# Four graph layers on one core: the y tiles of layer 0 in three long runs between inner products

## The chip, the cores and the metric

The kernel runs on one core of a Trainium2 chip, in one launch. The metric is the device time of that launch in microseconds (us). TensorE (PE) multiplies matrices; PEld is its loading of weights, which goes on beside the multiplications. VectorE (DVE), ScalarE (ACT) and GpSimd (POOL) work on elements. SyncE (SP) issues most of the DMAs. Each engine works through its own queue in order and waits on semaphores.

## The reference

x has 8 batches of 2048 nodes with 64 features; adj is a dense 2048 x 2048 matrix. Everything is float32. Four layers follow each other, each as `x = layernorm(x + layer(x, adj))`:

```python
# layer 0: for each node n its own weights, mixed from 16 sets by the node's embedding
w = einsum('nd,dkio->nkio', embedding, weight);  b = einsum('nd,do->no', embedding, bias)
As = [I, A, 2 * A @ A - I]
out = einsum('bnki,nkio->bno', einsum('knm,bmc->bnkc', stack(As), x), w) + b
# layer 1: twice  z = relu((A z) W_i)
# layer 2: x W_self + (A x) W_neighbor + bias
# layer 3: [x, A x, 2 A A x - x, A x, 2 A A x - x] W + bias
```

Every layer needs products with A, and layer 0 in addition needs for every node and batch a product with the 16 weight sets (`y` in the kernel), summed with the 16 numbers of the node's embedding.

## The kernel before

**Layout.** The tile `xy` in SBUF holds two slots of the node features: 128 partitions by 16 node tiles by 2 slots by 512 columns (8 batches of 64 features, in 4 pairs `p`). A first part (lines 500 to 715) computes A x for layer 0, puts it in slot 1, keeps its transpose in DRAM (`t1T`), and prepares sums of blocks of A for what follows (`comb`, in DRAM).

**A product with A.** From then on `product` does every product, six in all: layer 0's T2 = A (A x), then A z twice in layer 1, once in layer 2 and twice in layer 3. It is a Strassen-like scheme on two levels. The outer level has seven products of halves, named A11, S1, A12, S2, S4, S3, A22 in the order in which they run, on quarters of the features or on sums of them (`T`, made by `t1` to `t4`). Each of the seven is a call of `inner`, which has again seven block products (`mul`). A block product loads one 1 MB block of A or of its sums (`load`, tile `a`, a ring of four buffers; from layer 1's A12 on, three more in `ring2`, which lies in the memory that layer 0's tiles leave), and multiplies it in four matmuls of 128 x 128 by 128 x 512 into one PSUM bank: `mma`, `mmb` or `mmc`. There are two banks in layer 0, used in turn, so the third accumulation of an inner product takes the bank that the first has just left. VectorE adds the partial results: `u2`, `u3`, then the results (`C`), and before each inner product the four sums of its features (`t`).

**The y tiles.** T2's results come out in quarters: (0,0) after A12, (0,1) after S4, (1,1) after S3, (1,0) after A22, four tiles of 512 nodes by one pair of batches in each. As soon as a tile is there, `hand_over` gives a generator `feature0` (line 770) to the pump. For each of its four node tiles it runs two halves: 12 matmuls with 64 rows (the two batches of a pair side by side in the array) put 2 x 512 numbers into a PSUM tile `y` (three buffers). VectorE adds the first half's eight parts into `xy`, each scaled by the embedding (line 800); ScalarE scales the second half's eight parts into `s` (line 804); GpSimd sums them and adds the sum into `xy` (lines 809 and 811). `fetch` loads xT and tT of the tile ahead through SyncE's queue.

**Layer norm.** When two neighbouring pairs of a group of nodes are done, `then` puts the layer norm of these columns on a list of deferred work (`defer`, with a gap of 4 steps). It squares on GpSimd (`sq`, line 365), reduces on VectorE (`ss`, line 371), takes a square root on ScalarE (line 376) and scales `xy` (line 381).

**The pump.** `pump.step` is called after every block product and lets pending generators go on. For layer 0 the rate is 4 and the batch 16: after every four block products, 16 steps are done, which is two y tiles. `mark` notes the last tile of quarter (0,1); `pass_mark`, at the start of the next product, runs the pump to there. The tiles that are left run within layer 1's A11 and S1, after which `drain` empties the pump and `between` (`to_late`) frees layer 0's memory, PSUM included.

**What sets the order.** The program is written in one stream. A scheduler then gives each engine its order: by the place in the stream, but an instruction that is ready may go ahead of others that wait. `tc.keep_in_program_order` pins an instruction. Waits are put in after that.

Of the kernel before, what the change touches and what calls it, by code (L numbers as in the profile page):

```python
# [22 lines left out]
A11, A12, A22, S1, S2, S3, S4 = range(7)  # L23
# [6 lines left out]
class Pump:  # L30


    def __init__(self):
        self.jobs = []
        self.later = []
        self.rate = 1
        self.gate = None
        self.owed = 0
        self.batch = 1

    def add(self, gen):
        self.jobs.append(gen)
# [22 lines left out]
    def tick(self, idle=False):  # L65
        for job in list(self.later):

            job[0] -= 0.5 if idle and job[4] else 1
            if job[0] <= 0:
                job[0], job[4] = job[1], False  # L70
                if next(job[2], "done") == "done":
                    self.later.remove(job)

    def step(self, n=1, now=False):
        self.owed += n
        if self.jobs and self.owed < self.batch and not now:
            return
        n, self.owed = int(self.owed), self.owed - int(self.owed)
        while n > 0 and (self.jobs or self.later):
            try:  # L80
                idle = not self.jobs
                if not idle:
                    next(self.jobs[0])
                n -= 1
                self.tick(idle)
            except StopIteration:
                self.jobs.pop(0)
# [8 lines left out]
def kernel(  # L96
# [18 lines left out]
    nc = tc.nc  # L115
# [73 lines left out]
            nc.sync.dma_start(a, comb[q][s].rearrange("p (n m c) -> p n m c", n=TG, m=TG))  # L189
        return a  # L190

    def product(src, feature, between=None, rate=1, own=None, pin=False, batch=1):

# [8 lines left out]
        def new_t():  # L204
            return sums.tile([P, NT // 2, 4 * F], F32, tag="T", name="T", bufs=3)
# [4 lines left out]
        def inner(q, b, finish, early=None):  # L210


            b11, b12, b21, b22 = (
                b[:, hm * TG : (hm + 1) * TG, ts(hc, 2 * F)] for hm in range(2) for hc in range(2)
            )

            def new():
                return sums.tile([P, TG, 2 * F], F32, tag="t", name="t", bufs=5)

            t1 = add(new(), b12, b11, ALU.subtract)  # L220
            t2 = add(new(), b22, t1, ALU.subtract)
            t3 = add(new(), b22, b12, ALU.subtract)
            t4 = add(new(), b21, t2, ALU.subtract)

            def mul(ps, s, xb, start, stop=True):
                a = load(q, s)
                for m in range(TG):
                    nc.tensor.matmul(  # L228
                        ps, xb[:, m, :], a[:, :, m, :], start=(start and m == 0),
                        stop=(m == TG - 1), skip_group_check=True,  # L230
                    )
                pump.step(pump.rate)

            def bank(n):
                nonlocal banks
                banks += 1
                pool = p_mm if p_mm2 is None or banks % 3 else p_mm2
                return pool.tile([P, GW], F32, tag="mm", name=f"mm{n}")

            pa, pb = bank("a"), bank("b")  # L240
            mul(pa, 0, b11, True)
            p1 = sums.tile([P, GW], F32, tag="p1", name="p1")
            nc.scalar.copy(p1, pa)  # L243
            if early is not None:
                early(2, p1)
            mul(pb, 5, t2, True)
            u2 = add(sums.tile([P, GW], F32, tag="u2", name="u2"), pb, p1)
            if early is not None:
                early(1, u2)
            mul(pa, 1, b21, False)  # L250
            finish(0, pa, None)
            mul(pb, 6, t3, False)
            u3 = add(sums.tile([P, GW], F32, tag="u3", name="u3"), pb, p1)
            if early is not None:
                early(3, u3)
            pc = bank("c")
            mul(pc, 4, t1, True)
            finish(3, pc, u3)
            mul(pb, 3, t4, False)
            finish(2, pb, p1)  # L260
            mul(pc, 7, b22, False)
            finish(1, pc, u2)

        def fresh(c):
            def finish(blk, ps, plus):
                if plus is None:
                    nc.scalar.copy(c[:, blk, :], ps)
                else:
                    add(c[:, blk, :], ps, plus)
            return finish,  # L270

        def onto(c, base, give=None, then=None):

            def early(blk, plus):
                add(c[:, blk, :], base[:, blk, :], plus)

            def finish(blk, ps, plus):
                add(c[:, blk, :], ps, (base if plus is None else c)[:, blk, :])
                if give is not None:
                    hand_over(c, *give, blk)  # L280
                if then is not None:
                    then(blk)
            return finish, early
# [16 lines left out]
        if pin:  # L300
            tc.keep_in_program_order(sub)
        inner(A11, b11, *fresh(u))
        inner(S1, t1, *fresh(v))
        pump.drain()
        pump.rate, pump.batch = rate, batch
        if between is not None:
            between()
        t2 = new_t()
# [3 lines left out]
        prior(0, 0)  # L312
        c = new_c()
        inner(A12, b21, *onto(c, u, (0, 0)))
        t3 = new_t()
        sub = nc.vector.tensor_tensor(t3, b22, b12, ALU.subtract)
        if pin:
# [3 lines left out]
        prior(1, 0)  # L321
        c = new_c()
        inner(S2, t2, *onto(u, u, then=lambda blk: add(c[:, blk], u[:, blk], v[:, blk])))
        inner(S4, b22, *onto(c, c, (0, 1)))
        pump.mark()
        prior(1, 1)

# [2 lines left out]
            hand_over(v, 1, 1, blk)  # L330

        inner(S3, t3, *onto(u, u, then=last))
        inner(A22, t4, *onto(u, u, (1, 0)))

    def to_nodes(dst, pool, tiles, p, hT):
# [72 lines left out]
    if True:  # L408
# [347 lines left out]
        if True:  # L756
            p_y = first.enter_context(tc.tile_pool(name="p_y", bufs=3, space=PSUM))
            l0y = first.enter_context(tc.tile_pool(name="l0y", bufs=1))
            e_sb = l0y.tile([P, NT, D], F32, tag="e_sb", name="e_sb")
            nc.gpsimd.dma_start(e_sb, emb)  # L760


            order = [
                (2 * ih + k // 2, 2 * ch + k % 2)
                for ih, ch in ((0, 0), (0, 1), (1, 1), (1, 0)) for k in DONE
            ]
            fetched = {}

            def fetch(k):
                if k < len(order):  # L770
                    i, p = order[k]
                    fetched[i, p] = [l0y.tile([P, GW], F32, tag=n, name=n, bufs=2) for n in ("xT", "tT")]
                    for tile_, src in zip(fetched[i, p], (xT, t1T)):
                        nc.sync.dma_start(tile_, src[p][:, ts(i, GW)])

            def feature0(g, p, hT):
                if (g, p) == order[0]:
                    fetch(0)
                fetch(order.index((g, p)) + 1)
                terms = fetched.pop((g, p)) + [hT]  # L780
                for k in range(TG):
                    t = g * TG + k
                    acc = xy[:, t, 0, ts(p, 2 * F)].rearrange("p (b f) -> p b f", f=F)


                    s = l0y.tile([P, DH, 2, F], F32, tag="s", name="s", bufs=2)
                    for h in range(2):
                        y = p_y.tile([P, 2, DH * F], F32, tag="y", name="y")
                        for n in range(3):
                            for b in range(2):  # L790
                                half = slice(b * F, (b + 1) * F)
                                nc.tensor.matmul(  # L792
                                    y[:, b, :], terms[n][half, ts(k, P)],
                                    wn[half, n, h * DH : (h + 1) * DH, :],
                                    start=(n == 0), stop=(n == 2),
                                )
                        for d in range(DH):
                            e = e_sb[:, t, h * DH + d : h * DH + d + 1]
                            if h == 0:
                                nc.vector.scalar_tensor_tensor(  # L800
                                    acc, y[:, :, ts(d, F)], e, acc, ALU.mult, ALU.add
                                )
                            else:
                                nc.scalar.activation(s[:, d], y[:, :, ts(d, F)], AF.Copy, scale=e)  # L804
                        if h == 0:
                            yield
                    n = DH // 2
                    while n:
                        nc.gpsimd.tensor_tensor(s[:, :n], s[:, :n], s[:, n : 2 * n], ALU.add)  # L809
                        n //= 2  # L810
                    nc.gpsimd.tensor_tensor(acc, acc, s[:, 0], ALU.add)
                    yield

            product(1, then(feature0, 0, gap=4, pool_sq=True), rate=4, batch=16)


    late = p_z = None
# [134 lines left out]
```

## Time and profile before

Three runs took 1692.46, 1690.90 and 1686.34 us, median 1690.9. The profiled execution took 1690.62 us, its span from the first to the last instruction is 1688.8.

| | us | share of the span |
|---|---|---|
| time of the profiled execution | 1690.62 | |
| its span | 1688.8 | |
| TensorE busy | 1666.1 | 99% |
| weight loads | 856.5 | 51% |
| VectorE busy | 942.0 | 56% |
| ScalarE busy | 265.3 | 16% |
| GpSimd busy | 249.6 | 15% |
| y matmuls in the chain of waits | | 19.5% |
| matmuls of products (`mma`, `mmb`, `mmc`) in the chain | | 57.7% |

The granted clock of TensorE was 0.996 of full speed. The y tiles run between 225 and 752 us: the first part ends at about 220 us, layer 1's S1 begins at 752.

In the profile a line of the chain of waits has start, length, engine, tile and line of the kernel, and the number of records. One float32 matmul shows as two records, so a block product is x8, one y tile x96. A line of the timeline has start, length, engine, line, operation and shapes, and in brackets how long the engine had been idle and what ended it.

### The profile page before, as it was taken

The page shows a single profiled execution, that of the slowest core. Times are in us where ns is not written, and L with a number is a line of the kernel's source. Part 1 is how long each engine was busy: PE and PEld are TensorE (multiplying, and loading weights), DVE is VectorE, ACT ScalarE, POOL GpSimd, SP SyncE. Part 2 cuts the span into 40 slices and gives each one's busy share as a digit, 9 for nine tenths or more (in the row PEclk, how much of TensorE's full clock was granted, in tenths as well). Part 3 has the DMA queues.
Part 4 walks back from the last instruction along what each step waited for, and adds up shares of the span by engine and source line. Part 5 has one row for each costly group of instructions (what it writes and reads, how often), then busy time and mean ns, then how long its engine had stood idle before and what let it go on. Part 6 is the DMA issues. An engine that isn't in the chain of part 4 may idle for free.

```text
span 1688.8 us, 16180 instructions
## 1 busy us (share of the span) xinstructions
PE 1666.1 (99%) x5952; PEld 856.5 (51%) x5952; DVE 942.0 (56%) x1687; ACT 265.3 (16%) x763; POOL 249.6 (15%) x332
## 2 busy tenths in 40 slices
PE   9899999999999999999999999999999999999997
PEld 4588854444444444444455455554444455554443
DVE  5477884546456656454443365863557444543556
ACT  0000000332323332330011010220001011100001
POOL 1122200443344544450000000000000000000000
PEclk9999999999999999999999999999999999999999
DMA  9898978134333123309877877667888866678883
GB/s 326 328 353 329 331 275 303 62 123 166 109 114 123 52 86 125 112 19 376 303 268 264 310 253 257 226 216 283 291 296 282 306 210 237 231 265 309 316 310 121
DMA packets 82271, 391.25 MB, mean 232 GB/s; under 512 B 8880, under 2 KB 25264, under 8 KB 42640
## 3 DMA queue, kind: packets, MB, share of 16 engines
q1 hardware_dynamic: 69504, 346.78, 58.4%
q0 software_dynamic: 11248, 42.08, 6.5%
q10 hardware_dynamic: 1440, 1.35, 0.2%
q8 instruction: 48, 0.79, 0.2%
q14 instruction: 31, 0.25, 0.0%
HBM read 339.85 MB, written 50.33 MB: 231 GB/s over the span
## 4 chain that ended last, share of the span: by engine, by line
PE 95%; DVE 3%; DMA 1%; POOL 0%; ACT 0%; issue 0%; POOLq 0%; DVEq 0%
PE mmb L228 25%; PE y L792 20%; PE mmc L228 17%; PE mma L228 16%; PE ps_n L655 8%; PE ps_n L618 3%; PE z L840 2%; PE z L872 2%; DMA a<-in_slices 1%; PE pt L831 1%; PE pt L889 1%; DVE ss L371 0%; PE pt_n L339 0%; DVE xy L381 0%; DVE sm L355 0%; DVE xy L356 0%
## 5 line engine op out<-in xcount | busy, mean ns | idle before, releaser
L228 PE MATMUL mmb<-a,t 128*128 128x512 f32 x1008 | 454.9, 593 | 1.1 <-DVE xy L381 1.1
L228 PEld LDWEIGHTS mmb<-a,t 128*128 128x128 f32 x1008 | 188.7, 190 | 229.0 <-issue 224.7
L800 DVE SCALAR_TENSOR_TENSOR xy<-y,e_sb,xy 128x128 f32<-128x128 f32 x512 | 179.7, 351 | 137.5 <-PE y L792 121.6
L809 POOL TENSOR_TENSOR s<-s 128x512 f32<-128x512 f32 (+2 forms) x192 | 159.0, 828 | 339.5 <-ACT s L804 329.3
L804 ACT ACTIVATE s<-y,e_sb 128x128 f32<-128x128 f32 x512 | 138.9, 382 | 270.5 <-PE y L792 270.4
L228 PE MATMUL mma<-a,T 128*128 128x512 f32 x384 | 173.3, 594 | 0.0
L201 DVE TENSOR_TENSOR u<-mmb,p 128x512 f32<-128x512 f32 x84 | 58.0, 690 | 193.8 <-PE mmb L228 188.4
L228 PE MATMUL mmc<-a,t 128*128 128x512 f32 x336 | 151.7, 594 | 0.0
L792 PE MATMUL y<-wn,xT 64*128 64x512 f32 x512 | 133.1, 592 | 0.0
L228 PE MATMUL mma<-a,xy 128*128 128x512 f32 x288 | 130.4, 594 | 2.7 <-DVE C L201 2.6
L792 PE MATMUL y<-wn,tT 64*128 64x512 f32 x512 | 131.3, 589 | 0.0
L792 PE MATMUL y<-wn,C 64*128 64x512 f32 x512 | 131.2, 589 | 0.0
L228 PEld LDWEIGHTS mma<-a,T 128*128 128x128 f32 x384 | 71.4, 190 | 84.3 <-issue 83.5
L201 DVE TENSOR_TENSOR C<-mmc,C 128x512 f32<-128x512 f32 x60 | 41.4, 690 | 101.7 <-PE mmc L228 101.7
L228 PEld LDWEIGHTS mmc<-a,t 128*128 128x128 f32 x336 | 61.9, 190 | 70.9 <-issue 70.4
L228 PEld LDWEIGHTS mma<-a,xy 128*128 128x128 f32 x288 | 53.8, 190 | 68.6 <-issue 62.9
L228 PE MATMUL mmc<-a,T 128*128 128x512 f32 x192 | 86.4, 593 | 0.0
L243 ACT COPY p<-mma 128x512 f32<-128x512 f32 x42 | 24.5, 584 | 377.8 <-PE mma L228 375.8
L792 PEld LDWEIGHTS y<-wn,xT 64*128 64x128 f32 x512 | 49.2, 187 | 63.3 <-issue 62.9
L792 PEld LDWEIGHTS y<-wn,tT 64*128 64x128 f32 x512 | 49.5, 187 | 60.6 <-issue 60.6
L792 PEld LDWEIGHTS y<-wn,C 64*128 64x128 f32 x512 | 49.6, 187 | 60.3 <-issue 60.3
L228 PE MATMUL mmc<-a,xy 128*128 128x512 f32 x144 | 64.9, 593 | 0.0
(114 smaller groups left out, 1587.9 us busy)
## 6 DMA issues: line engine op xcount, KB each, us to landing
a<-comb SPq DMA_DIRECT2D x240, 1024.0 KB, 4.8
a<-in_blocks SPq DMA_DIRECT2D x54, 1024.0 KB, 4.9
comb<-si POOLq DMA_DIRECT2D x28, 1024.0 KB, 10.9
a<-in_slices SPq DMA_DIRECT2D x15, 1024.0 KB, 8.2
comb<-so POOLq DMA_DIRECT2D x16, 512.0 KB, 5.7
comb<-so POOLq DMA_DIRECT2D x16, 256.0 KB, 5.6
t1T<-hT SPq DMA_DIRECT2D x16, 256.0 KB, 4.6
xT<-in_xT SPq DMA_DIRECT2D x16, 256.0 KB, 3.1
```

Of the source, the lines that this page charges most:

```text
L201: nc.vector.tensor_tensor(out, a, b, op)
L228: nc.tensor.matmul(ps, xb[:, m, :], a[:, :, m, :], start=(start and m == 0), stop=(m == TG - 1), skip_group_check=True,)
L243: nc.scalar.copy(p1, pa)
L618: mm = nc.tensor.matmul(ps[p], xcol(0, TG * j + m, p), ch[j][:, m], start=(j == 0 and m == 0), stop=(j == NG - 1 and m == TG - 1), skip_gr ...
L655: nc.tensor.matmul(ps[:, ts(p, GW // 2)], b(k, p), a(k // TG, k % TG), start=(start and p == k == 0), stop=(k == NT // 2 - 1), skip_group_ ...
L792: nc.tensor.matmul(y[:, b, :], terms[n][half, ts(k, P)], wn[half, n, h * DH : (h + 1) * DH, :], start=(n == 0), stop=(n == 2),)
L800: nc.vector.scalar_tensor_tensor(acc, y[:, :, ts(d, F)], e, acc, ALU.mult, ALU.add)
L804: nc.scalar.activation(s[:, d], y[:, :, ts(d, F)], AF.Copy, scale=e)
L809: nc.gpsimd.tensor_tensor(s[:, :n], s[:, :n], s[:, n : 2 * n], ALU.add)
L831: nc.tensor.transpose(pt[:, ts(k, P)], xy[:, g * TG + k, slot, ts(p, 2 * F)], ident)
L840: nc.tensor.matmul(z[:, k, :], aT[:, ts(k, P)], wd[:, w, :], start=(n == 0), stop=(n == len(terms) - 1),)
L872: nc.tensor.matmul(z[n][:, k], xT[half, ts(k, P)], w[half], start=True, stop=True)
```

## The change

The pump loses `batch` and gets `hold`: while it is set and jobs are pending, `step` does nothing. A new `run(n)` takes the first n jobs and runs them to their ends, one after the other. `product` takes `runs`, which says after which inner product how many tiles are run: four after S2 (quarter (0,0)) and four after S3 (quarter (0,1)). The eight tiles of (1,1) and (1,0) are all run after A11 of layer 1, in `product`'s next call, which then ends the hold. The first y matmul of each node tile is pinned in program order.

```diff
+    def run(self, n=None):
+
+        while self.jobs and n != 0:
+            for _ in self.jobs[0]:
+                self.tick()
+            self.jobs.pop(0)
+            n = None if n is None else n - 1
+
     def step(self, n=1, now=False):
+        if self.jobs and self.hold and not now:
+            return
         self.owed += n
-        if self.jobs and self.owed < self.batch and not now:
-            return
...
-    def product(src, feature, between=None, rate=1, own=None, pin=False, batch=1):
+    def product(src, feature, between=None, rate=1, own=None, pin=False, runs=None):
...
         inner(A11, b11, *fresh(u))
+        if pump.hold:
+            pump.run()
+            pump.hold = False
         inner(S1, t1, *fresh(v))
         pump.drain()
-        pump.rate, pump.batch = rate, batch
+        pump.rate, pump.hold = rate, runs is not None
+        runs = runs or {}
...
         inner(A12, b21, *onto(c, u, (0, 0)))
+        pump.run(runs.get(A12, 0))
...
         inner(S2, t2, *onto(u, u, then=lambda blk: add(c[:, blk], u[:, blk], v[:, blk])))
+        pump.run(runs.get(S2, 0))
         inner(S4, b22, *onto(c, c, (0, 1)))
+        pump.run(runs.get(S4, 0))
...
         inner(S3, t3, *onto(u, u, then=last))
+        pump.run(runs.get(S3, 0))
         inner(A22, t4, *onto(u, u, (1, 0)))
...
-                                nc.tensor.matmul(
+                                mm = nc.tensor.matmul(
...
+                                if n == b == h == 0:
+                                    tc.keep_in_program_order(mm)
...
-            product(1, then(feature0, 0, gap=4, pool_sq=True), rate=4, batch=16)
+            RUNS = {S2: NP, S3: NP}
+            product(1, then(feature0, 0, gap=4, pool_sq=True), rate=4, runs=RUNS)
```

`NP` is 4. In the order in which the program is built, TensorE's work in layer 0 and at the start of layer 1 becomes: A11, S1, A12, S2, four y tiles, S4, S3, four y tiles, A22, then layer 1's A11, eight y tiles, S1. Before, it was A11, S1, A12, then two y tiles after every four block products, the last two ahead of the last block product of layer 1's A11; two single y matmuls stood within the first A11.

More of the change, by code (lines that the diff above doesn't have):

```diff
@@ L38, in __init__ @@
         self.owed = 0
-        self.batch = 1
+        self.hold = False
     def add(self, gen):
```

## The prediction

> **What bounds the kernel now.** I read the page first, then the windows by stage, then who waits for whom on TensorE, then the chain of waits and the timeline around the y tiles.
>
> ```profile
> PE 1666.1 (99%) x5952; PEld 856.5 (51%) x5952; DVE 942.0 (56%) x1687; ACT 265.3 (16%) x763; POOL 249.6 (15%) x332
> ...
> 225.00:752.00 527.00, 524.37 (x1979) 231.22 (x1978) 300.93 (x676) 146.40 (x527) 201.04 (x259) 1.00 0.36 124
> ...
> 240.00:297.00 57.00, 57.00 (x134) 25.08 (x132) 32.43 (x34) 1.75 (x3) 0.00 (x0) 1.00 0.88 305
> ```
>
> The columns of a window are its length, then busy time of PE, PEld, DVE, ACT and POOL, the granted clock, the DMA share and GB/s. TensorE is busy 99% of the span, and in the stretch that holds every y tile (225 to 752 us) it misses only 2.6 of 527 us. So a change of order can win no more than TensorE's idle time there, plus what TensorE loses inside its busy time by going back and forth between two kinds of work. The third line is a stretch of bare block products: TensorE never idle, DMA at 0.88.
>
> The waits of TensorE between 225 and 770 us are two:
>
> ```profile
> PE mma L228 <- DVE C L201: 2.6, 1, 2.6
> PE mmb L228 <- DVE xy L381: 1.1, 1, 1.1
> ```
>
> The chain shows what going back and forth costs, and where the first wait comes from:
>
> ```profile
> 226.24 1.05 PE y L792 x2
> 227.29 1.05 PE mma L228 x2
> ...
> 402.16 1.90 POOL sq L365
> 404.06 0.02 issue
> 404.09 1.23 DVE ss L371
> ...
> 405.80 0.56 DVE C L201
> 406.36 0.04 issue
> 406.40 3.70 PE mma L228 x8
> ...
> 430.71 41.40 PE y L792 x192
> 472.11 3.63 PE mma L228 x8
> 475.74 3.43 PE mmb L228 x8
> ```
>
> A block product (8 records) takes 3.43 us, but 3.63 directly after y tiles: 0.20 us for each way back. Two y tiles take 41.40 us, 20.70 each; entering costs nothing visible. A single y matmul that was hoisted alone (226.24, again at 234.35) takes 1.05 us. The 2.6 us wait is a layer norm: VectorE stands at the reduction `ss` until GpSimd has squared (404.06), and behind it in VectorE's queue stands the add that frees the PSUM bank of the next product.
>
> The second wait I don't take at its word:
>
> ```profile
> 755.97 0.45 POOL L811 TENSOR_TENSOR xy<-xy,s 128x128 f32<-128x128 f32 x1
> ...
> 756.45 6.60 SPq L189 DMA_DIRECT2D a<-comb  x5
> ...
> 763.84 3.67 PE L228 MATMUL mmb<-a,t 128*128 128x512 f32 x8 [1.14 <-DVE xy L381]
> ```
>
> SyncE issues nothing until 756.45, just after GpSimd's last add into xy: the first load that goes into layer 0's freed memory (`ring2`) stands in SyncE's queue ahead of S1's fourth adjacency block. That block was issued right behind it, seven microseconds before the product that uses it began. The late one is the DMA; VectorE's layer norm only ended at the same moment.
>
> **What the Trainium skill says.** "TensorEngine Tiling (Array Packing)", Key Properties: changing the tiling mode drains TensorE. The y matmuls use 64 rows, the block products 128; the trace agrees as to the way back (0.20 us) and shows nothing on the way in. "SBUF — State Buffer", SBUF: two separate sides: a VectorE operation with two SBUF inputs and a GpSimd operation lock each other out. The trace agrees: the three sums of s take 2.6 us alone and 3.48 us beside VectorE's adds. "Perfetto Trace Analysis", Identifying Dependency Chains: an instruction with several waits gets separate wait instructions in front; so a gap can carry the name of one semaphore and belong to another, as I read the second wait. "DMA: Bandwidth & Descriptors", Where 436 GB/s comes from: HBM gives one core about 358 GB/s; the bare stretch at 305 GB/s and 0.88 share (305/0.88 = 347 at full share, an estimate from the window) fits.
>
> **The change part by part.** No instruction of arithmetic is added or removed. The built order is the same on every engine from S1's end in layer 1 on; GpSimd's order is the same throughout.
>
> *Fewer ways back.* Before: eight runs of two tiles and two single matmuls, ten ways back. After: three runs (4, 4 and 8 tiles), three ways back. 7 x 0.20 = 1.4 us.
>
> *The two hoisted matmuls* are now held in place. They took 2 x 1.05 = 2.10 us; as part of a run their four records cost 4 x 41.40/192 = 0.86. Gain 1.24 us.
>
> *The first stall (2.63 us).* Call T the end of a y run. From before's first long stall (T = 393.2): VectorE ends its last y work at T+0.6 and the first layer norm at T+4.4; ScalarE's last eight copies end at T+4.8; GpSimd's sums at T+8.9, its square at T+10.85. After the change the second layer norm of quarter (0,0) falls into S4's start, ahead of the add that frees S4's first bank. Reduction, scale, reciprocal: T+12.6; that add ends at T+13.15 (all of these as in the chain above). The product that needs the bank is S4's fifth, at T + 3.63 + 3 x 3.43 = T+13.92. Slack 0.8 us: no stall. Before, the run ended in mid-product and the freed bank was wanted 10.3 us after T; now a run ends before an inner product, whose first products need nothing from VectorE but sums made earlier. Next late is u3 (T+15.8, wanted T+17.35).
>
> *After the second run* the other layer norm is recorded only when layer 1 begins: about 3.9 us of VectorE and 2.3 for the T sum behind A22's last add, done 7 us into A11; A11's u2, next in the queue, ends about 8.4 us in and is wanted at 10.3. No stall.
>
> *Third run.* Two layer norms stand inside it; a y half takes 2.59 us on TensorE, with 3.05 (VectorE) or 2.17 (ScalarE) of 5.17 per pair behind it, and three y buffers. The delay of 3.8 us makes the next use of a buffer 0 to 0.25 us late; before had such norms within its runs, still at 41.40, so I take 0.
>
> *Second stall (1.14 us) stays.* The ring2 load still waits for GpSimd's last add at T+7.7 (756.42 - 748.7), and S1's fifth block stands behind it. Before, one product of A11 and four of S1 separated T from the late one (its fourth); the ring then held three of S1's blocks. Now it holds four, and the fifth is wanted at the same T+13.92. Same issue, same loads in flight: 1.14 us again, between 0 and 2.
>
> *DMA.* Before, bare stretches were 21 products at the start; now 28, then 14 and 14. Ring of four: a block is freed three products (10.3 us) before it is wanted, and lands in 4.9 us (median in the bare stretch, longest 7.3). xT/tT fetches stand behind four prefilled blocks and ahead of the fifth, which can't be issued before TensorE's first product after the run anyway. Cost 0.
>
> Sum: 1.4 + 1.24 + 2.63 = 5.27 us off 1690.6 (the profiled execution: span 1688.8 and 1.8 around it) gives 1685.4; off the median 1690.9, 1685.6. Forecast 1685.5.
>
> **Rivals.** (1) The first stall only moves into S4: if GpSimd's square is over 0.8 us later than in before, the excess is back, up to 2.6. For it: the slack is thin and the lock between VectorE and GpSimd can shift it; against: the neighbours are the same. 1690.8 - 2.64 = 1688. (2) The S1 stall goes too, because its fifth load is served sooner: 6.4 us in all, 1684.4. Against: geometry unchanged. This is also the ceiling, but for the three ways back that remain. (3) Slower: bare stretches fall under DMA's rate. Place: the 28, 14 and 14 products that no y tile relieves any more; need 1.049 MB per 3.43 us = 306 GB/s. If only 290 GB/s came, each would take 3.62 us, 56 x 0.19 = 10.6 less 5.3 gained: +5, 1696. It decides from about 298 GB/s down. For it: the share of 0.88, and that the y stage ran at 99 GB/s and left room. Against: 57 us at 305 GB/s with TensorE full and no growing lateness.
>
> **How the numbers follow.** Forecast 0.69, (1) 0.14, (2) 0.08, (3) 0.09. The three times of before spread over 6 us, so I put 3 us on either side of a median. Range 1681 to 1691.5: forecast and both neighbours with that spread; left out is most of (3). Half a per cent (8.5 us) is what a measurement of this kernel can tell from no change: below 1682.4 or above 1699.4. The forecast lies 3 us inside the first bound: faster 0.14 (spread, and case 2), slower 0.06 (the upper part of 3), within 0.80.
>
> **What would show it.** Three y runs of 82.8, 82.8 and 165.6 us in the chain, each followed by one 3.63; the first beginning near 319 us and S1 of layer 1 near 746.7 (before 752.2); no wait of mma on a C add; one wait of about 1.1 us on S1's fifth product, with SyncE's issue at T+7.7. Wrong: products of 3.5 us and more in the bare stretches (3), a wait on mmc in S4 (1), a y run longer than 20.7 us a tile.

## The result, and the profile after

| | before | after |
|---|---|---|
| median of 7 runs each (lowest to highest), us | 1690.9 (1686.34 to 1692.46) | 1683.36 (1680.82 to 1684.08) |
| span of the profiled execution, us | 1688.8 | 1679.1 |
| from the end of the first part to the start of the fifth block product in layer 1's S1, us | 546.72 | 541.28 |

The ratio is 0.9953, with a 95% interval of 0.994 to 0.9967. The forecast was 1685.5 us, the range 1681 to 1691.5.

The page and the waits of TensorE in after (us in total, times, longest):

```profile
PE 1661.4 (99%) x5952; PEld 856.3 (51%) x5952; DVE 939.3 (56%) x1687; ACT 265.6 (16%) x763; POOL 246.6 (15%) x332
...
PE ps_n L672 <- DMA a<-in_slices: 1.8, 1, 1.8
PE mmc L237 <- DMA a<-comb: 1.2, 1, 1.2
...
PE mma L237 <- ACT p L252: 0.7, 1, 0.7
```

The 2.6 us wait on a C add has gone. One wait of 1.2 us remains at S1's fifth product, now under its own name, the adjacency block's DMA. A 0.7 us wait on ScalarE is new. The chain of waits of after has the three runs, with start and length in us:

```profile
311.85 3.43 PE mmc L237 x8
315.28 82.60 PE y L809 x384
397.88 3.63 PE mma L237 x8
...
446.15 82.60 PE y L809 x384
528.75 3.63 PE mma L237 x8
...
577.01 162.45 PE y L809 x756
742.54 1.14 DVE ss L388
```

Four y tiles take 82.60 us, not twice 41.40. Bare block products take 3.43 us.

**A part of the difference arises before the change.** These are windows of the same three stages, first of before, then of after (columns as in the prediction: length, busy time of PE, PEld, DVE, ACT, POOL, clock, DMA share, GB/s). The first ends where the chain of waits passes to the DMA of `in_slices` that TensorE comes to wait for, the second where this wait ends, the third where the last eight transpose records ahead of A11 begin:

```profile
0.00:60.95 60.95, 58.84 (x145) 28.23 (x146) 36.51 (x41) 3.04 (x4) 11.85 (x22) 1.00 0.95 349
60.95:77.59 16.64, 11.18 (x76) 9.39 (x75) 2.27 (x9) 1.66 (x3) 0.18 (x1) 0.90 0.85 297
77.59:220.79 143.20, 143.19 (x678) 125.77 (x679) 110.95 (x163) 7.52 (x13) 31.72 (x46) 0.99 0.90 331
```

```profile
0.00:61.32 61.32, 59.21 (x145) 28.32 (x146) 36.68 (x41) 3.04 (x4) 12.07 (x22) 1.00 0.96 355
61.32:74.36 13.04, 11.19 (x77) 9.41 (x76) 2.00 (x8) 1.66 (x3) 0.00 (x0) 1.00 0.96 341
74.36:215.86 141.50, 141.50 (x678) 124.59 (x679) 110.91 (x163) 7.53 (x13) 31.81 (x46) 1.00 0.91 335
```

The first part ends at 220.79 us in before and at 215.86 in after, although every engine has the same instructions in the same order up to there. So 4.93 of the 9.7 us between the spans arise before the first instruction that the change moves. The last section takes this part up. The rest is 5.44 us gained from there to S1's fifth block product, with 0.7 given back after it (9.7 - 4.93 - 5.44). In what follows I compare kernels by this stretch, called *the stretch*: from the start of the last eight transpose records before A11 to the start of S1's fifth product in layer 1, the first into `mmc`.

The end of the stretch favours after a little. There the fifth product itself has waited and takes 3.67 us, 0.24 more than a bare one, which falls behind the end. In before the wait is one product earlier, and its 0.24 lies inside. To the end of the fifth product the gain is 550.15 - 544.95 = 5.20 us, and 0.4 us are given back after that.

### The profile page after: what moved, and what is told of

Read it like the earlier page. It is cut to its first block, busy times and chain, and to the rows that moved or that the text cites. A ratio compares the mean times of both kernels' runs of the same rounds, so it can differ in the third digit from the quotient of the medians.

```text
span 1679.1 us, 16179 instructions
## 1 busy us (share of the span) xinstructions
PE 1661.4 (99%) x5952; PEld 856.3 (51%) x5952; DVE 939.3 (56%) x1687; ACT 265.6 (16%) x763; POOL 246.6 (15%) x332
## 4 chain that ended last, share of the span: by engine, by line
PE 95%; DVE 3%; DMA 1%; issue 0%; POOL 0%; ACT 0%; SPq 0%; POOLq 0%
PE mmb L237 25%; PE y L809 20%; PE mmc L237 17%; PE mma L237 16%; PE ps_n L672 8%; PE ps_n L635 3%; PE z L861 2%; PE z L893 2%; PE pt L852 1%; PE pt L910 1%; DMA a<-in_slices 1%; DMA a<-comb 0%; PE pt_n L356 0%; DVE ss L388 0%; DVE sm L372 0%; DVE xy L373 0%
```

## The experiments

All keep the whole computation. c_before, c_after, b_pin and a_ringpin ran on one chip, b_pin_b8, b_pin_b4, b_pin_gap12 and a_best on another, b_pin_b64 and a_nopin on a third, each time beside the kernel before. "b" kernels start from before, "a" kernels from after.

**Unchanged copies: c_before and c_after.** How far do time and stretch repeat?

> The kernel before, unchanged, once more. Both theories: a ratio of 1.000 to itself. It is here for its trace. Theory 'order alone' (what the change gains lies between 220 and 770 us; the start differs only by chance): the first part, up to the last eight transposes before A11, takes anything between 215 and 221 us, the stretch from there to S1's fifth block product (in S1 the second mmc-bank product's start, 546.7 us in the first profile of before) again 546 to 547 us. Theory 'the start is faster too': first part again close to 220.8 us, as in the first profile.

> The changed kernel, unchanged, once more. Theory 'order alone': the stretch from the end of the first part to S1's fifth block product again about 541.3 us, 5.4 less than before; the first part anywhere between 215 and 221; ratio 0.9955 to 0.998. Theory 'the start is faster too': first part again close to 215.9 us while before's is close to 220.8, ratio near 0.9945.

Measured: c_before 1.0002 of before (0.9992 to 1.0011), stretch 546.75; c_after 0.9959 (0.9947 to 0.9971), stretch 541.22. The stretch repeats to 0.06 us, while the end of the first part came at 219.44 and 215.71. The change is worth 546.73 - 541.25 = 5.5 us in the stretch, and 5.2 to 5.3 to the end of the fifth product. Of 1690.9 us, 5.5 are a ratio of 0.9968: inside c_after's interval, 0.0001 outside that of the first comparison. What the medians show beyond it, some 1 to 2 us, must lie outside the stretch. The first part ended between 215.7 and 220.8 us over twelve traces, and not by kernel alone: a_nopin, with after's order of runs, had 219.53, and b_pin_b64, with before's scheme, 216.16. The last section shows that most of the excess goes with the granted clock; why the clocks differed stays open.

**b_pin: the two hoisted matmuls alone.** Before, with the first matmul of each tile pinned as in after:

```diff
-                                nc.tensor.matmul(
+                                mm = nc.tensor.matmul(
...
+                                if n == b == h == 0:
+                                    tc.keep_in_program_order(mm)
```

> The kernel before with the first y matmul of each node tile pinned, so that none is hoisted into A11; runs of two tiles as before. If the two hoisted matmuls cost what the sum of the prediction says, 1.24 us net and 0.4 for their two ways back: about 1.3 to 1.6 us less, the trace from 220 us on showing it before 240 us and the stalls of 2.6 and 1.1 us still there. Rival: the pin also lets other work slip, and nothing or less than 0.5 us is gained.

Measured: 1.0001 (0.9991 to 1.0011), stretch 546.30, only 0.43 us below before's. TensorE's waits in the stretch show where the rest went:

```profile
PE mma L228 <- DVE C L201: 2.6, 1, 2.6
PE mmb L228 <- DMA a<-comb: 1.1, 1, 1.1
...
PE mma L228 <- ACT p L243: 0.7, 1, 0.7
```

The last line is new: TensorE waits where a hoisted y matmul had stood. ScalarE had not yet copied out (to `p`) the PSUM bank that the next product needs, and the single matmul had filled that hole. From the end of the first part to the end of the product behind the second single, before took 239.03 - 220.79 = 18.24 us and after 232.88 - 215.86 = 17.02. Of this gain of 1.22 us the four records cost 0.86 again within a run, which leaves 0.4. The same edit shows by its absence too, in a_nopin below. In this run the wait of 1.1 us also has its right name, the DMA, with nothing done to it; c_before, the unchanged copy, still names VectorE's `xy`.

**b_pin_b8 and b_pin_b4: the cost of a run, in two doses.** b_pin with a batch of 8 and of 4, that is 16 runs of one tile and 32 of half a tile in place of 8 of two.

```diff
-            product(1, then(feature0, 0, gap=4, pool_sq=True), rate=4, batch=16)
+            product(1, then(feature0, 0, gap=4, pool_sq=True), rate=4, batch=8)
```

> As b_pin, but the batch is 8: one y tile after every two block products, sixteen runs where b_pin has eight. The stretch from the end of the first part to S1's fifth block product was 546.3 us in b_pin. If a y run costs 0.4 us beside its tiles (0.2 on the way in, 0.2 on the way back), 8 x 0.4 = 3.2 us more, 549.5, apart from waits, which the trace names. If only the way back costs (0.2, as the prediction had it), 547.9.

> As b_pin, but the batch is 4: half a y tile after every block product, 32 runs. With 0.4 us for each run 24 x 0.4 = 9.6 us more than b_pin, 555.9 in the same stretch, apart from waits; with 0.2, 551.1.

Measured (one execution each): 1691.24 and 1696.71 us, beside a median of 1690.48 for before. The stretches are 548.1 and 553.8. The waits of b_pin_b8 in it:

```profile
PE mma L228 <- ACT p L243: 2.4, 2, 1.7
...
PE y L792 <- DVE xy L802: 0.4, 1, 0.4
```

Both long waits of b_pin are gone, and a 1.7 us wait on ScalarE has come. Net of waits, b_pin's stretch is 546.3 - 4.4 = 541.9, b_pin_b8's 548.1 - 2.8 = 545.3 and b_pin_b4's 553.8 - 2.4 = 551.4: 3.4 us for 8 more runs and 9.5 for 24 more, which is 0.43 and 0.40 for each run. The way back (0.20) is half of it. The other half is the way in. It shows in the lengths of runs: one tile takes 20.80 us (chain of b_pin_b8, below), two take 41.40 and four 82.60, and both 2 x 20.80 - 41.40 and 2 x 41.40 - 82.60 are 0.20. In after's timeline (start, length) it is spread over the last product and the first records of a run:

```profile
288.36 20.80 PE y L792 x96
```

```profile
311.69 3.60 PE L237 MATMUL mmc<-a,T 128*128 128x512 f32 x8
315.21 1.13 PE L809 MATMUL y<-wn,xT 64*128 64x512 f32 x4
316.18 1.02 PE L809 MATMUL y<-wn,tT 64*128 64x512 f32 x4
317.04 1.02 PE L809 MATMUL y<-wn,C 64*128 64x512 f32 x4
```

From the product's start to the first y record are 3.52 us where bare products follow each other at 3.43, and from there to the next four records 0.97 where the later ones follow at 0.86: 0.09 and 0.11 more.

Is it the number of rows that costs, or any change between two kinds of matmul? The `z` matmuls of layer 1 have 128 rows like the block products. In the chain of after:

```profile
781.41 0.89 PE z L861 x8
782.30 3.44 PE mmc L237 x8
```

The product after them takes 3.44 us, only 0.01 more than a bare one. So not every change costs 0.20. That the 64 rows are the cause is likely; no run here changes the rows alone.

**b_pin_gap12: does the first stall come from where the layer norm falls?** b_pin with the norm recorded 12 steps after its tile, not 4.

```diff
-            product(1, then(feature0, 0, gap=4, pool_sq=True), rate=4, batch=16)
+            product(1, then(feature0, 0, gap=12, pool_sq=True), rate=4, batch=16)
```

> As b_pin (runs of two tiles), but a layer norm of layer 0 is put off by 12 steps in place of 4, so that VectorE no longer stands at GpSimd's square ahead of an add that frees a PSUM bank. If that is the cause of the 2.6 us stall: the wait of mma on a C add is gone and the stretch is 2.9 us shorter (2.6 of wait and about 0.25 that a product takes longer after one), 543.4. If the runs of two tiles themselves make the stall: it stays or turns up elsewhere, 545.5 to 547.

Measured (one execution): 1692.97 us, but the stretch is 542.07, 4.2 us shorter than b_pin's. The 2.6 us stall is gone, so it was the norm's place. The other wait has gone as well: S1's adjacency block came in time. The two waits with the slower product after each are 2.63 + 0.27 + 1.09 + 0.24 = 4.23 us. Why S1's wait went shows on ScalarE, first of before, then of this run:

```profile
750.95 0.22 ACT L376 ACTIVATE rs<-rs 128x16 f32<-128x16 f32 x1 [5.03 <-DVE rs L375]
```

```profile
745.53 2.17 ACT L806 ACTIVATE s<-y,e_sb 128x128 f32<-128x128 f32 x8 [2.98 <-PE y L792]
```

In before a norm's square root, which waits for VectorE, stands in ScalarE's queue ahead of the last scalings; ScalarE is idle for 5.03 us. With the norm put off it is idle for only 2.98. The loads that SyncE issues behind GpSimd's last add go out 2.1 us after S1's start, where in before it was 4.2. The price is later. TensorE's wait in layer 1's A12, from the timeline, and VectorE's last norm ahead of it:

```profile
777.65 5.37 PE L228 MATMUL mma<-a,xy 128*128 128x512 f32 x8 [4.58 <-issue]
...
776.32 1.22 DVE L381 TENSOR_TENSOR xy<-xy,rs 128x1024 f32<-128x1024 f32 x1
```

The product reads `xy` of quarter (1,0), whose norm ends at 777.54; it starts 0.11 us later, after 4.6 us of waiting. It also takes 5.37 us, where a product behind a wait of 1.1 us takes 3.67: the granted clock was 0.83 from 775 to 785 us. "issue" in the brackets means that the trace names no releaser; the operand does.

**a_ringpin: is S1's wait the DMA behind ring2's load?** After, with the first ring2 load pinned, so that SyncE issues it in program order, behind the S1 block that it had overtaken:

```diff
-            nc.sync.dma_start(a, comb[q][s].rearrange("p (n m c) -> p n m c", n=TG, m=TG))
+            d = nc.sync.dma_start(a, comb[q][s].rearrange("p (n m c) -> p n m c", n=TG, m=TG))
...
+        if ring2 is not None and loads == RING + 1:
+            tc.keep_in_program_order(d)
```

> The changed kernel with the first load into ring2 pinned in program order, so that SyncE no longer holds S1's fifth block behind it. Theory 'the 1.2 us wait is that DMA': the wait of mmc on the load of a in S1 is gone, nothing new in its place, 1.2 us less from 740 us on. Rival 'VectorE's layer norm': the wait stays at 1.1 to 1.2 us. Against the kernel before 0.994 to 0.997.

Measured: 0.9957 of before (0.9945 to 0.9969), stretch 540.08, 1.2 us below after's. First the chain of after at this place, then that of a_ringpin:

```profile
742.54 1.14 DVE ss L388
...
744.19 0.04 ACT rs L393
...
744.32 2.17 ACT s L823 x8
746.55 1.28 POOL s L828
...
749.23 0.47 POOL xy L830
749.72 0.32 SPq L197
...
750.09 6.92 DMA a<-comb
...
757.14 3.67 PE mmc L237 x8
```

```profile
744.53 3.63 PE mma L239 x8
748.16 3.43 PE mmb L239 x8
751.60 3.43 PE mma L239 x8
755.03 3.43 PE mmb L239 x8
758.46 3.43 PE mmc L239 x8
```

In after, ScalarE's last scalings, GpSimd's sums, SyncE's issue and 6.92 us of DMA follow one another up to the product. With the load in program order S1's five products stand back to back, and no other wait takes the place of the 1.2 us. The norm whose scaling (`xy`, line 381) the trace of before had named is still there and holds up no product. An earlier norm has a part, though: its reduction on VectorE and its square root on ScalarE stand at the head of after's chain, ahead of the last scalings, as in before (b_pin_gap12). Either remedy takes the wait away: that norm later, or the load in order.

**a_best: two runs of 8 tiles, with a_ringpin's load.**

```diff
-            RUNS = {S2: NP, S3: NP}
+            RUNS = {S3: 2 * NP}
```

> The changed kernel with the ring2 load pinned, and two runs of eight tiles (after S3 and after layer 1's A11) in place of 4, 4 and 8. One run less: 0.4 us, in the stretch 540.1 - 0.4 = 539.7, if the layer norms at the end of the first long run stall nothing. Rival: four layer norms close to A22 and A11 now delay an add there and cost 1 us or more. Against the kernel before 0.9945 to 0.997.

Measured: 0.9957 (0.9944 to 0.9971), stretch 540.34. One run fewer should have gained 0.4; a wait of y on VectorE's add, where a norm and a sum of features stand between the adds of the first long run, took it:

```profile
PE y L811 <- DVE xy L821: 0.4, 1, 0.4
```

So it is no better than a_ringpin. Neither can be told from after by its total time.

**b_pin_b64: three runs in other places.** Batch 64 gives runs of 5, 8 and 3 tiles wherever the count is reached. In the trace only the first stands within an inner product, after S4's fifth block product. The second stands between A22 and layer 1's A11, the third after S1, directly ahead of layer 1's A12. So it tests less of the place in mid-product than its expectation says.

```diff
-            product(1, then(feature0, 0, gap=4, pool_sq=True), rate=4, batch=16)
+            product(1, then(feature0, 0, gap=4, pool_sq=True), rate=4, batch=64)
```

> As b_pin, but the batch is 64: three y runs, of five, eight and three tiles, as few as in the changed kernel, but in the middle of inner products (the first before S2's second to last block product's neighbour, the last within layer 1's S1). Count alone: 5 x 0.4 = 2.0 us less than b_pin in the stretch (546.3): 544.3. If only the place between inner products takes the 2.6 us stall away, a wait of mma or mmc on a C add of some 2 to 3 us is still there. If the stall goes with the count, 541.4. First part: if it depends on the order of the later program, near 217 us as in the kernels made from the changed one; if it is chance, anything from 215.7 to 220.8.

Measured: 1.0084 (1.0069 to 1.0099), 14 us slower with as many runs as after. The timelines show the end of it (VectorE, then TensorE):

```profile
781.58 1.22 DVE L371 TENSOR_REDUCE ss<-sq 128x16 f32<-128x1024 f32 x1 [5.39 <-POOL sq L365]
784.21 1.22 DVE L381 TENSOR_TENSOR xy<-xy,rs 128x1024 f32<-128x1024 f32 x1
785.53 5.76 PE L228 MATMUL mma<-a,xy 128*128 128x512 f32 x8 [13.63 <-issue]
```

After the last y tile come ScalarE's scalings, GpSimd's sums and square and the norm, and A12 needs the result: TensorE waits 13.6 us, until 0.10 us after the norm's end. I had expected a stall of another kind, on a C add; there is none. Another wait of 3.7 us stands within the second run, where a norm and layer 1's sums of features come between VectorE's y adds. What counts besides the number of runs is how much work on A separates the last y tile from the first reader of its norm. In after these are S1's seven products.

**a_nopin: after without the pin** on the first matmul of a tile.

```diff
-                                if n == b == h == 0:
-                                    tc.keep_in_program_order(mm)
```

> The changed kernel without the pin: three runs between inner products, but two y matmuls hoisted into A11 as before. The stretch (541.25 in the changed kernel): 0.45 us more, 541.7, as b_pin against before showed; the prediction's sum would have had 1.6 more, 542.9. First part as in the other kernels made from the changed one, 215.7 to 218.4, if it depends on the later order.

Measured: 0.9963 (0.995 to 0.9977), stretch 541.63. That is 0.4 us above after's, as the pin was worth in b_pin.

## Why the prediction was right, step by step

The prediction's 5.27 us stand against 5.5 measured in the stretch, and against 5.2 to 5.3 to the end of S1's fifth product. That they meet so closely is in part luck: two terms were wrong by about 1 us each, with opposite signs.

| step | predicted | measured | by |
|---|---|---|---|
| the two hoisted matmuls, with their ways back | 1.24 + 0.4 | 0.4 | b_pin, a_nopin |
| five runs of tiles fewer | 1.0 | 2.0 | b_pin_b8, b_pin_b4 |
| the first stall | 2.63 | 2.9 | b_pin_gap12; its wait is absent in after |
| S1's wait | 0 | 0 | it stays, 1.2; a_ringpin removes it |
| sum | 5.27 | 5.3 | 5.20 between before and after, 5.29 between the copies, to the end of the fifth product |

- **The hoisted matmuls** were costed as if nothing stood behind them. They filled a wait for ScalarE's copy of a bank, and the prediction did not ask what would be waited for once they were gone.
- **"Entering costs nothing visible"** was wrong: 0.2 us, the same as the way back. It is inside the 41.40 us of a two-tile run, which the prediction divided by two. The Trainium skill ("TensorEngine Tiling (Array Packing)", Key Properties) says that a change of the tiling mode drains TensorE; the traces now show 0.2 us in each direction. The prediction's reading that they show nothing on the way in does not hold.
- **The first stall** went, and nothing came in its place. It was worth 0.27 us more than its wait, since the product after it took 3.70 us and not 3.43. The timing in S4 came out nearly as worked out. In VectorE's timeline of after, with T = 397.88:

```profile
408.93 1.22 DVE L388 TENSOR_REDUCE ss<-sq 128x16 f32<-128x1024 f32 x1 [1.79 <-POOL sq L382]
...
410.56 0.63 DVE L210 TENSOR_TENSOR C<-mma,C 128x512 f32<-128x512 f32 x1
...
412.86 0.68 DVE L210 TENSOR_TENSOR u<-mmb,p 128x512 f32<-128x512 f32 x1
```

  The norm's reduction begins at T+11.05 (predicted 10.85), the add that frees the bank ends at T+13.3 (13.15), and the product starts at 411.81 = T+13.93 (13.92). u3, the next add, ends at T+15.66 (15.8). The slack is 0.6 us where 0.8 was predicted. Rival (1), the stall moving into S4, did not happen, by that margin.
- **S1's wait** was read rightly as the DMA behind the ring2 load, against the name that the trace of before gave. It stayed, so rival (2) did not happen; a_ringpin shows that it could be had. What holds GpSimd's last add back, the earlier norm ahead of ScalarE's last scalings, the prediction did not name.
- **Rival (3)**, bare stretches under the DMA's rate, is refuted: the products of these stretches take 3.43 us. The two stretches of 14 products last 48.27 and 48.26 us, which is 3.63 + 13 x 3.43 each. TensorE is busy 464.69 of 465.89 us from the start of S2 to S1's fifth product, and the 1.2 us that it misses there are S1's wait.
- **The landmarks** hold once the 4.93 us of the first part are added to after's times: the first run begins at 315.28 + 4.93 = 320.2 (predicted 319; the 1.2 us between them are the gain from the hoisted matmuls that did not come), S1 at 741.94 + 4.93 = 746.9 (746.7). Each run is followed by one product of 3.63 us.

The median came out 2.1 us below the forecast. At most 0.2 of this are the sum. Most of the rest goes with the granted clock of the runs (last section), which was not in the sum.

## What to carry to other kernels

Before costing the removal of work that an engine does out of turn, ask what it would wait for in that place; the gain is the work less that wait. The price of switching between two kinds of work is best taken from runs of different lengths (here one of four against two of two), because the half on the way in hides in the run's own mean. When work is gathered into few long runs, look at what is queued behind the end of each run and who reads the last result: with three runs in both, it cost nothing to have S1's seven products behind the last one, and a wait of 13.6 us to have A12 there.

## What the runs showed that I had not expected

**The medians differ by more than the stretch, and so do the clocks.** In the first part TensorE waits once for `in_slices`, in before from 72 to 78 us. These are the windows from 70 to 90 us of before, of a_best and of after (the clock is the third number from the end):

```profile
70.00:90.00 20.00, 14.53 (x68) 12.20 (x67) 14.22 (x26) 2.70 (x5) 5.09 (x8) 0.83 0.68 232
```

```profile
70.00:90.00 20.00, 18.11 (x84) 15.40 (x84) 16.84 (x30) 2.83 (x5) 5.50 (x9) 0.91 0.74 254
```

```profile
70.00:90.00 20.00, 18.15 (x92) 15.70 (x91) 17.36 (x33) 2.83 (x5) 6.06 (x9) 1.00 0.76 264
```

Of the twelve traces, before and b_pin_gap12, where the wait took 5.5 and 4.7 us, have 0.83 here; after, c_after and b_pin_b64, with 1.8, 2.2 and 1.5 us, have 1.00; the other seven, with 1.9 to 3.5 us, have 0.91. Where the clock stays at 1.00 the rest of the first part takes 141.5 us, and in the others 143.0 to 143.6. The eight matmul records behind the wait take 1.99 us at 1.00, and 2.8 to 3.8 in the others. Long waits thus go with a lower clock, and the wait costs more than itself. The length of the wait alone does not decide: c_after with 2.2 us kept its clock, a_best with 1.9 did not, and behind before's stall of 2.6 us at 404 us the clock is 1.00 and the product takes 3.70 us.

Each run's mean clock over its whole span is on record too. At 0.997, 27 runs of before and c_before average 1689.1 us and 6 of after and c_after 1683.7; at 0.998, 5 runs average 1686.4 and 4 runs 1681.2. So at the same clock the change is worth 5.4 and 5.3 us, close to the stretch's gain. (At 0.996 it is 6.6, with only two runs of the changed kernel. A thousandth of the clock is about 1.7 us of 1690, so this comparison is coarse.) But 31 of those 63 runs of the kernel before stood at 0.996 or lower, and only 2 of the 12 of the changed kernel. The means are 0.9963 and 0.9972; the difference is some 1.5 us, an estimate that takes the whole span as bound by TensorE, and as much as the medians show beyond the stretch. Whether the change has a part in the clock, these runs don't show: the instructions up to the end of the first part are the same.

**DMA above the figure that the prediction cited.** It cited the Trainium skill ("DMA: Bandwidth & Descriptors", Where 436 GB/s comes from) for about 358 GB/s from HBM for one core. Between 759 and 765 us of before, the DMA engines moved 416 GB/s on average. The measurement decides: that figure was no bound here, and rival (3) had more room than it seemed.
